# A four-layer network on one core: order of the row blocks in the third layer of the first image, and the place of the second layer of the last image

## The chip, the cores and the metric

The kernel runs on one core of one Trainium2 chip. The metric is the device time of one execution in microseconds (us). Three executions of the kernel before took 2457.15, 2460.21 and 2460.98 us; their median, 2460.21, is the time before.

## The reference

The input is `x`, four images (B = 4) of 64 x 64 places with 64 channels, f32. Four layers follow one another, each of them taking the output of the one before. Cut to what matters:

```python
# layer 0: attention over the 4096 places of an image
q, k, v = x @ Wq + bq, x @ Wk + bk, x @ Wv + bv          # 4096 x 64 each
attn = softmax(einsum('bic,bjc->bij', q, k))             # 4096 x 4096
x = gamma * einsum('bmn,bmc->bnc', attn, v) + x

# layer 1: a gated convolution block
y = dw3x3(pw1(layernorm(x)))                             # 64 -> 256 channels, 3 x 3 per channel
y = y1 * y2                                              # halves of the channels, 128
y = y * (mean(y over places) @ sca_w + sca_b)
x = x + pw2(y) * beta                                    # 128 -> 64
z = pw3(layernorm(x)); z = z1 * z2
x = x + pw4(z) * gamma

# layer 2: attention, on the image read as one matrix without weights
xf = x.reshape(B, C, N)
attn = softmax(einsum('bci,bcj->bij', xf, xf))           # 4096 x 4096, symmetric before the softmax
x = einsum('bcj,bij->bci', xf, attn) + x

# layer 3: attention with 32 inner channels, then a batch norm over all images
f = softmax(theta(x) @ phi(x).T); w_y = (f @ g(x)) @ w_W + w_b
x = x + gamma * (w_y - mean(w_y)) * rsqrt(var(w_y) + eps) + beta    # mean and var over B, H, W
```

## The kernel before

All four images stay on the chip in one array `X` (128 partitions). The program takes its ordinary path in one pass; a second path is there for values out of range only and isn't taken here. The order of the work is written out by hand. `items` is the list of all steps in order: 32 for each image's layer 0, 100 for layer 2 of image 0, 72 for layer 2 of each other image, 64 for each image's layer 3. `due` holds functions that are called after a given item (`at(i, fn)`). Two lanes, `conv` and `misc` (class `Lane`, L995), hold generators; each `yield` names an estimate in us, and `tick(us)` lets the generators go on when their estimated time has come. `run()` (L1831) goes through the items and ticks the lanes. So a lane decides how densely foreign work is put between the steps: each instruction of it stands in its engine's queue behind what was issued before. On TensorE (PE), ScalarE (ACT), VectorE (DVE) and GpSimd (POOL) the program's order is the engine's order; the order of SyncE (SP), which issues most of the DMAs, is left to the tile scheduler.

Layer 1 is the generator `layer1(b)` in the lane `conv`. It starts 34 items after layer 0 of image b has started, so that layer 1 of images 0, 1 and 2 lies beside layer 0 of the next image, and that of image 3 beside layer 2 of image 0. Its parts in order: the first norm (`norm`: squares L1164 on ACT, sums over channels L1170 on PE, L1175, L1176, L1178 and L1179 on ACT and DVE, eight DMAs L1183, a multiplication L1191); twice, for each half of the channels, the first pointwise product (L1205 on PE, L1222 on ACT) into the padded image `pad`, and the convolution in four groups of nine taps, each a 128 x 1024 instruction (L1236 on ACT for the first tap of image 3, L1240 and L1243 on DVE, a product of the halves L1251); the channel weights (L1260); the second pointwise product (L1269 on PE, L1274, L1276); the second norm; the third (L1205, L1286, L1288) and fourth (L1292, L1293, L1295). What follows the taps, from the second norm on, is called the tail of layer 1 below.

Layer 2 (`layer2`, L1322) takes the 4096 x 4096 scores in 8 x 8 blocks of 512. Since the matrix is symmetric, the exponentials of a block serve twice: once for the row block h that is being worked on, and, transposed, for the row block g. PE makes scores from the keys `ko`, which `features2` (L1300) has prepared from X (transposes L1307 on PE, copies L1310 on DVE and ACT, DMAs L1311). One step covers half a block: the score L1384 on PE, two exponentials L1389 on ACT into an `e` buffer, and two or three steps later the products L1440 on PE into two PSUM accumulators. At the end of a row block the accumulators are added to `A` (L1448, L1451, L1454). In a step that belongs to a pair of blocks, `turned` also transposes the exponentials on DVE (L1402) into a buffer `turned`, and `column_sums` adds them up on POOL (image 0: by DMAs that accumulate, L1417; other images: by additions, L1419); the rest is in L1421, L1429 and L1430. When the pair's four steps are done, a *run* follows (`turned_products`): 128 matmuls (L1465) of the turned exponentials with `xr`, a rearranged part of X that `weights` (L1361) has loaded by 16 DMAs of 32 KB, and four additions to `A` (L1478, L1480). The order of row blocks, and where the pairs lie in each, stands in two lists. `FULL`, for images 1 to 3, has 14 runs in 72 steps. `PART`, for image 0, has 7 runs in 100 steps: it works through more blocks directly and turns fewer. In `PART` the runs end at steps 7 and 15, and then, after the 52 steps that hold the row blocks 1 to 4 and most of 7, at 67, 75, 83, 91 and 97. All 100 steps tick the lane `conv` by 3.1 us.

What comes between layer 2 and layer 3 of an image is `close2` (L1517: the sums are gathered and inverted, and A is scaled and added to X), in five turns that are put at given steps of the next image's layer 2; then `open3` (L1560, the projections of layer 3) and `keys3` (L1599, 16 DMAs L1605). Layer 3 (L1610) follows: scores L1627, exponentials L1638, sums L1658 to L1679, products L1688, and `close` (L1744), which writes `wy`; that of images 0 and 1 is kept in the buffer of `pad`.

Buffers: `big` has five (q, v, yg, ko, A, turned and others), `e` six of 2048 columns (two steps each), `t` two, `xn` one (the norms' y and z, xr of images 1 to 3), `pad` one. [...]in layer 2, three slots of two banks go round (`new_ps`, and `piece` for single turns), the fourth holds the accumulators (`new_acc`). A new tile in a buffer waits until the readers of the old one are done.

Of the kernel before, what the change touches and what calls it, by code (L numbers as in the profile page):

```python
# [8 lines left out]
F32 = mybir.dt.float32  # L9
# [682 lines left out]
def fast_path(ctx: ExitStack, tc: tile.TileContext, a: dict, out: bass.AP, bad):  # L692
# [11 lines left out]
    xn = ctx.enter_context(tc.tile_pool(name="xn", bufs=1))  # L704
# [31 lines left out]
    def piece():  # L736
        if turn_of["banks"]:
            return PS[:, bass.ts(new_bank(), 512)]
        return new_ps()[:, 0:512]
# [8 lines left out]
    def new_e(name="e"):  # L748
        return ep.tile([128, 2048], F32, tag="e", name=name)
# [4 lines left out]
    def new_big(name):  # L754
        return big.tile([128, 4096], F32, tag="big", name=name)

    def new_pad(name="pad"):
        return big.tile([128, 66 * PW + 2], F32, tag="pad", name=name, bufs=1)
# [80 lines left out]
    for nm in names64 + names32:  # L839
        n = flat[nm].shape[0]  # L840
# [151 lines left out]
    def at(i, fn):  # L992
        due.setdefault(i, []).append(fn)
# [25 lines left out]
    conv, misc = Lane(), Lane()  # L1019
# [5 lines left out]
    im = [Image() for _ in range(B)]  # L1025
# [49 lines left out]
    between, late, steps, LAG = [], [], [], 6  # L1075
# [5 lines left out]
    def follow(lag=LAG):  # L1081
        if len(late) > lag:
            late.pop(0)()
# [215 lines left out]

    def features2(b):  # L1300
        x = X[:, b]
        im[b].ko = ko = new_big("ko")
        kv = ko[:, 0:N].rearrange("p (a e n) -> p a e n", e=2, n=128)
        for g in range(4):
            ps = piece()
            for i in range(4):
                nc.tensor.transpose(ps[:, bass.ts(i, 128)], x[:, bass.ts(4 * g + i, 128)], ident)  # L1307
            for e, copy in enumerate((nc.vector.tensor_copy, nc.scalar.copy)):
                own, other = slice(64 * e, 64 * e + 64), slice(64 - 64 * e, 128 - 64 * e)
                copy(kv[own, bass.ts(g, 4), e, :], ps[own, :].rearrange("p (a n) -> p a n", n=128))  # L1310
                nc.sync.dma_start(out=kv[other, bass.ts(g, 4), e, :], in_=kv[own, bass.ts(g, 4), e, :])  # L1311
            yield 3.5
# [1 line left out]
    SIDES = [[(7, (h + 1) % 7), ((h + 2) % 7, (h + 3) % 7)] for h in range(7)]  # L1314
    FULL = [(7, [7])] + [(h, [h] + SIDES[h]) for h in range(6)] + [(6, SIDES[6] + [6])]
    PART = [
        (0, [0, 5, (1, 2), 6, 7, (3, 4)]), (1, [1, 2, 3, 4, 7]), (2, [2, 1, 3, 4, 7]), (3, [3, 1, 2, 4]),
        (4, [4, 1, 2, 3]), (7, [7, 0, 5, 6, 1, 2, (3, 4)]), (6, [6, 0, (1, 2), 5, 7, (3, 4)]),
        (5, [5, 0, (1, 2), 6, (3, 4), 7]),
    ]  # L1320

    def layer2(b, when_free=None):  # L1322
# [5 lines left out]
        steps, runs = [], []  # L1328
# [16 lines left out]
        st = {"e": {}, "T": {}, "esum": {}}  # L1345

        def tile_of(run):
            return run % 2 if b else run // (len(runs) - 1)

        def slot(g, t):  # L1350
            k = used[g, t] = used.get((g, t), -1) + 1
# [2 lines left out]

        def weights(h):
            if "xr" not in st:
                st["xr"] = new_e("xr") if b == 0 else xn.tile([128, 2048], F32, tag="xn", name="xn")
            for q in range(4):
                for k in range(4):
                    c = 1024 * (h % 2) + 256 * k  # L1360
                    nc.sync.dma_start(  # L1361
                        out=st["xr"][32 * q : 32 * q + 32, c : c + 256],
                        in_=x[32 * k : 32 * k + 32, 256 * h : 256 * h + 256],
                    )

        if b == 0:
            weights_at = {0: 0, 24: 7, 44: 6, 74: 5}
        else:
            weights_at = {6: 0, 8: 1, **{mine[h][0] - 1: h for h in range(2, 7)}}

        def score(n):
            h, g, u, _, _ = steps[n]
            if n == 0:
                if b > 1:
                    take_slots(0, 1, 2)
                m.zs = sm.tile([128, 216], F32, tag="zs2", name="zs2")
            if n % 2 == 0:
                st["pair"] = new_e()
            e = st["e"][n] = st["pair"][:, bass.ts(n % 2, 1024)]
            ps = new_ps()  # L1380
            for r, c in quads:
                rows_ = slice(64 * r, 64 * r + 64)
                k = 512 * g + 256 * u + 128 * r + 64 * c
                mm(  # L1384
                    ps[64 * c : 64 * c + 64, bass.ts(r, 512)], m.ko[rows_, k : k + 64],
                    m.ko[rows_, bass.ts(h, 512)], start=True, stop=True,
                )
            for r in range(2):
                act(  # L1389
                    e[:, bass.ts(r, 512)], ps[:, bass.ts(r, 512)], AF.Exp, bias=SHIFT2,  # L1390
                    accum_out=slot(g, 2 * u + r),
                )

        def turned(n):
            _, _, _, run, ti = steps[n]
            if run is None:
                return
            k = tile_of(run)
            if k not in st["T"]:
                st["T"][k] = new_big("turned")  # L1400
            T = st["T"][k].rearrange("p (e s j) -> p s e j", e=16, s=8)
            nc.vector.transpose(  # L1402
                T[:, 2 * ti : 2 * ti + 2], st["e"][n].rearrange("p (s e i) -> p s e i", s=2, e=16)
            )

        def column_sums(n):
            h, _, _, run, _ = steps[n]
            if run is None:
                return
            k, e = mine_t[h].index(n), st["e"][n]  # L1410
            if k == (0 if b == 0 else 1):
                st["esum"][h] = new_e("esum")
            if h not in st["esum"]:
                return
            esum = st["esum"][h][:, 0:1024]
            if b == 0:
                nc.gpsimd.dma_start(out=esum, in_=e, **({} if k == 0 else {"accum_op": ALU.add}))  # L1417
            else:
                nc.gpsimd.tensor_add(esum, st["e"][mine_t[h][0]] if k == 1 else esum, e)  # L1419
            if n == mine_t[h][-1]:  # L1420
                nc.gpsimd.tensor_add(esum[:, 0:512], esum[:, 0:512], esum[:, 512:1024])  # L1421

        def spread_sums(h):
            if h == m.mirrored[0]:
                m.cs = sm.tile([128, 128], F32, tag="cs2", name="cs2", bufs=1)
                if b == 0:
                    nc.gpsimd.memset(m.cs, 0.0)
            esum = st["esum"][h]
            nc.vector.transpose(esum[:, 512:1024], esum[:, 0:512])  # L1429
            nc.vector.tensor_reduce(  # L1430
                m.cs[:, bass.ts(h, 16)], esum[:, 512:1024].rearrange("p (e j) -> p e j", j=32), AX.X, ALU.add
            )
# [50 lines left out]
        def item(n):  # L1483
            if n in weights_at:
                weights(weights_at[n])
            score(n)
            turned(n)
            column_sums(n)
            todo.append(n)
            if n == 2:  # L1490
                m.A = new_big("A")
            if b == 0:
                follow(0)
                conv.tick(3.1)
                misc.tick(1.8)
            if n >= late_start:
                for _ in range(2):
                    if todo and todo[0] <= n - (3 if b == 0 and todo[0] in begin else 2):
                        products(todo.pop(0))
            for run, (_, _, last) in enumerate(runs):  # L1500
                if n - (3 if b and run == 0 else 2) == last:
                    turned_products(run)
                    if run == len(runs) - 2 and when_free:
                        when_free()
            if n == len(steps) - 1:
                while todo:
                    products(todo.pop(0))
            if n in spread_at:
                spread_sums(spread_at[n])

        for n in range(len(steps)):
            items.append((lambda n=n: item(n), 1.6 if b else 0.0))
# [281 lines left out]
    conv_from, misc_from, misc_to = {}, {}, {}  # L1794
# [9 lines left out]
    for b in range(B):  # L1804
        misc_to[len(items)] = True
        f = len(items)
        if b == 0:
            layer2(b)
            misc_from[f + 74] = [features2(b + 1)]
        else:  # L1810
            layer2(b, lambda b=b: keys3(b - 1))
            turns = close2(b - 1)
            for i in (8, 12, 22, 32, 42):
                at(f + i, lambda turns=turns: next(turns))
            misc_from[f + 46] = [open3(b - 1)]
            f = len(items)
            misc_to[f] = True
            layer3(b - 1)
            if b + 1 < B:
                turns = features2(b + 1)  # L1820
                for i in (4, 7, 10, 13):
                    between3[f + i] = 2, lambda turns=turns: next(turns)
    f = len(items)
# [220 lines left out]
```

## Time and profile before

| what | value |
|---|---|
| median of three executions | 2460.21 us |
| the profiled execution | 2460.18 us, of which the span of its core is 2458.3 us; mean granted TensorE clock 0.996 |
| PE, 27509 matmuls | 2414.6 us busy |
| DVE, ACT, POOL | 1471.1, 1648.8 and 528.0 us busy |
| 0 to 30 us: load and set-up | 24.0 us PE |
| 30 to 1031: layer 0, with layer 1 of images 0 to 2 | 996.6 us PE, 425.9 DVE, 669.4 ACT |
| 1031 to 1292: layer 2 of image 0, with layer 1 of image 3 | 245.2 us PE, 166.3 DVE, 168.2 ACT, 31.4 POOL |
| 1292 to 1470: layer 2 of image 1 | 177.9 us PE, 119.1 DVE, 82.3 ACT, 121.7 POOL |
| 1470 to 1610: layer 3 of image 0 | 139.0 us PE, 114.6 DVE, 130.7 ACT |
| 1610 to 1790: layer 2 of image 2 | 179.7 us PE, 126.7 DVE, 88.3 ACT, 116.7 POOL |
| 1790 to 2458: the rest | 652.2 us PE, 508.5 DVE, 498.9 ACT, 217.2 POOL |

How to read it. "Busy" is the time in which an engine carries out instructions; a wait is the idle time ahead of an instruction, put down to what released it last. A line of the waits names the engine, what it writes and the line of the program that waited, then, behind an arrow, the engine, its output and the line that it waited for; the three numbers are the us in all, how many times, and the longest one. In a timeline, each line has the start in us, the busy time, engine, line, operation, output and inputs by their names, the size of the tile, and the number of instructions that are taken together; in brackets is the idle time ahead of it and its releaser. In a row of windows, the stretch is followed by its length and by the busy time of each engine with the number of instructions. The tenths of the page cut the span into 40 equal slices of 61.5 us.

### The profile page before, as it was taken

Reading aid. Unit: us, or ns where it says so; the run is one execution under the profiler, and the core shown is the slowest. Engines: PE = TensorE matmul, PEld = TensorE weight load, DVE = VectorE, ACT = ScalarE, POOL = GpSimd, SP = SyncE. Lnnn points to the kernel's source line nnn. Section 1 sums busy time; section 2 is a strip of 40 time slices with the busy share of each in tenths; the row PEclk is TensorE's granted clock in tenths of the full one; section 3 lists DMA queues with packets and bytes.
Section 4 is the critical chain, followed back from the end, with each engine's and each line's share of the span. In section 5 each row is a group of like instructions: output and inputs, shape, how many; then the busy total and the mean of one; then the engine's idle time right before and its main releaser. Section 6 shows DMA issues by size and latency. Waiting matters only on the chain.

```text
span 2458.3 us, 63648 instructions
## 1 busy us (share of the span) xinstructions
PE 2414.6 (98%) x27509; PEld 932.0 (38%) x27509; DVE 1471.1 (60%) x1785; ACT 1648.8 (67%) x3144; POOL 528.0 (21%) x379
## 2 busy tenths in 40 slices
PE   9999999999999999999899999999999999999998
PEld 3343453336433633335334442144431244421113
DVE  2010377227822773278547757877668876678886
ACT  4666766676666666678454449964479844579996
POOL 2000000000000000000127662247631365622110
PEclk9999999999999999999999999999999999999999
DMA  3000000000000000230540017610065400296554
GB/s 79 1 18 1 19 1 18 18 19 1 18 18 18 2 19 18 50 65 18 112 102 22 19 45 155 135 31 19 20 138 118 91 19 20 68 174 139 121 117 117
DMA packets 67094, 134.31 MB, mean 55 GB/s; under 512 B 12941, under 2 KB 34166, under 8 KB 66806
## 3 DMA queue, kind: packets, MB, share of 16 engines
q0 software_dynamic: 23744, 84.46, 17.2%
q1 hardware_dynamic: 42309, 43.85, 7.9%
q8 instruction: 218, 3.57, 0.6%
q10 hardware_dynamic: 752, 1.85, 0.2%
q14 instruction: 71, 0.57, 0.1%
HBM read 4.80 MB, written 4.19 MB: 4 GB/s over the span
## 4 chain that ended last, share of the span: by engine, by line
PE 85%; DVE 7%; ACT 4%; DMA 2%; issue 1%; SPq 0%; POOL 0%; ACTq 0%; DVEq 0%; POOLq 0%
PE PS L1121 18%; PE PS L1095 18%; PE PS L1384 9%; PE PS L1440 9%; PE PS L1627 8%; PE PS L1688 8%; PE PS L1465 7%; PE PS L1205 2%; DVE tg L1679 2%; DVE y L1240 2%; ACT e L1638 2%; DMA xn<-e 1%; ACT e L1389 1%; DVE turned L1402 1%; ACT e L1100 1%
## 5 line engine op out<-in xcount | busy, mean ns | idle before, releaser
L1100 ACT ACTIVATE e<-PS 128x1024 f32<-128x1024 f32 x512 | 523.6, 1023 | 332.3 <-PE PS L1095 299.6
L1389 ACT ACTIVATE e<-PS 128x512 f32<-128x512 f32 x632 | 370.8, 595 | 350.8 <-PE PS L1384 330.6
L1121 PE MATMUL PS<-e,vq 64*64 64x512 f32 x4096 | 577.2, 592 | 0.0
L1095 PE MATMUL PS<-X,q 64*64 64x512 f32 x4096 | 574.9, 590 | 1.8 <-DVE X L979 1.7
L1638 ACT ACTIVATE e<-PS 128x512 f32<-128x512 f32 (+2 forms) x588 | 500.1, 921 | 58.3 <-PE PS L1627 35.8
L1679 DVE TENSOR_TENSOR tg<-tg,e 128x2048 f32<-128x2048 f32 x172 | 393.9, 2290 | 42.8 <-ACT e L1638 31.4
L1384 PE MATMUL PS<-ko 64*64 64x512 f32 x2528 | 343.4, 596 | 2.9 <-DVE A L1480 2.0
L1440 PE MATMUL PS<-e,X 64*64 64x512 f32 x2528 | 339.7, 594 | 1.4 <-DVE X L1133 0.6
L1240 DVE SCALAR_TENSOR_TENSOR y<-pad,vec,y 128x1024 f32<-128x1024 f32 x240 | 307.9, 1283 | 14.8 <-ACT y L1236 7.4
L1419 POOL TENSOR_TENSOR esum<-esum,e 128x1024 f32<-128x1024 f32 x126 | 298.9, 2372 | 49.3 <-ACT e L1389 42.3
L1402 DVE STREAM_TRANSPOSE turned<-e 128x1024 f32<-128x1024 f32 x196 | 241.0, 1238 | 114.0 <-ACT e L1389 114.0
L1627 PE MATMUL PS<-tg,ph 32*64 32x512 f32 x4096 | 294.9, 612 | 1.4 <-ACT e L1638 1.2
L1417 POOL DMA_DIRECT2D esum<-e x28 | 23.1, 827 | 1222.3 <-ACT e L1389 1171.4
L1095 PEld LDWEIGHTS PS<-X,q 64*64 64x64 f32 x4096 | 184.0, 133 | 258.9 <-issue 178.5
L1121 PEld LDWEIGHTS PS<-e,vq 64*64 64x64 f32 x4096 | 184.1, 133 | 252.0 <-issue 158.7
L1688 PE MATMUL PS<-e,tg 128*32 128x512 f32 x2048 | 272.5, 604 | 0.0
L1108 DVE TENSOR_REDUCE sums<-zs 128x1 f32<-128x4 f32 x128 | 19.6, 153 | 260.6 <-ACT e L1100 260.4
L1440 PEld LDWEIGHTS PS<-e,X 64*64 64x64 f32 x2528 | 105.6, 134 | 171.2 <-issue 148.3
L1660 POOL DMA_DIRECT2D xn<-e x116 | 101.1, 897 | 289.9 <-ACT e L1638 205.0
L1384 PEld LDWEIGHTS PS<-ko 64*64 64x64 f32 x2528 | 98.0, 133 | 164.3 <-issue 135.2
L1465 PE MATMUL PS<-turned,xn 32*64 32x256 f32 x5376 | 156.3, 377 | 0.5 <-DVE sums L1534 0.5
L1627 PEld LDWEIGHTS PS<-tg,ph 32*64 32x64 f32 x4096 | 63.4, 129 | 222.5 <-ACT e L1638 191.5
(217 smaller groups left out, 1685.0 us busy)
## 6 DMA issues: line engine op xcount, KB each, us to landing
xn<-e POOLq DMA_DIRECT2D x132, 512.0 KB, 5.2
esum<-e POOLq DMA_DIRECT2D x28, 512.0 KB, 4.6
xn<-X SPq DMA_DIRECT2D x336, 32.0 KB
xn<-t SPq DMA_DIRECT2D x64, 128.0 KB
ph<-tg SPq DMA_DIRECT2D x64, 128.0 KB
ko<-ko SPq DMA_DIRECT2D x32, 128.0 KB
xr<-in_x_dram SPq DMA_DIRECT2D x13, 256.0 KB
q<-q SPq DMA_DIRECT2D x12, 256.0 KB
```

Source lines behind the costliest of these rows:

```text
L1095: mm(ps[64 * c : 64 * c + 64, bass.ts(r, 512)], m.q[rows_, 128 * t + 64 * c : 128 * t + 64 * c + 64], x[rows_, bass.ts(g, 512)], start=Tru ...
L1100: act(es[g // 2][:, bass.ts(g % 2, 1024)], ps, AF.Exp, bias=SHIFT0, accum_out=zs[:, g : g + 1],)
L1121: ins = mm(PS[64 * s : 64 * s + 64, 2048 + 512 * j : 2560 + 512 * j], vq[rows_, :], es[j // 2][rows_, k : k + 512], start=t == 0 and i < 2 ...
L1240: stt(y1, win, wt, y1, ALU.mult, ALU.add)
L1384: mm(ps[64 * c : 64 * c + 64, bass.ts(r, 512)], m.ko[rows_, k : k + 64], m.ko[rows_, bass.ts(h, 512)], start=True, stop=True,)
L1389: act(e[:, bass.ts(r, 512)], ps[:, bass.ts(r, 512)], AF.Exp, bias=SHIFT2, accum_out=slot(g, 2 * u + r),)
L1440: mm(st["acc"][r][64 * c : 64 * c + 64, :], xw[rows_, 4 * g + 2 * u + c, :], st["e"][n][rows_, bass.ts(c, 512)], start=n == mine[h][0], st ...
L1465: mm(slots[q // 2][64 * c : 64 * c + 64, o : o + 256], st["xr"][rows_, w : w + 64], T[rows_, bass.ts(e, 256)], start=e < 2, stop=e >= 14,)
L1627: mm(PS[64 * c : 64 * c + 64, bass.ts(banks[k], 512)], m.ph[32 * k : 32 * k + 32, 128 * mc + 64 * c : 128 * mc + 64 * c + 64], m.th[32 * k ...
L1638: act(e[:, 512 * lo : 512 * k], PS[:, 512 * banks[lo] : 512 * banks[lo] + 512 * (k - lo)], AF.Exp,)
L1679: nc.vector.tensor_add(esum, esum, e)
L1688: mm(st["y"][32 * k : 32 * k + 32, :], m.gx[:, i % 32, :], es[i][:, bass.ts(k, 512)], start=mc == 0, stop=i % 32 == 31,)
```

## The change

Eight edits, all in layer 2 and what lies around it:

1. `ko` of image 1 is put into the buffer of `pad`, not into a `big` buffer.
2. `PART` has a new order: row blocks 0, 1, 7, 2, 6, 3, 5, 4 in place of 0, 1, 2, 3, 4, 7, 6, 5. The parts of each row stay as they are. The 7 runs now end at steps 7, 15, 41, 59, 67, 83 and 89: row blocks with pairs (0, 7, 6, 5) have a row block without any (1, 2, 3, 4) between them.
3. The `turned` tiles of image 0 alternate from run to run, as they do for the other images. Before, the first six runs took one tile and the seventh another.
4. `xr` of image 1 takes an `e` buffer, like that of image 0, and not `xn`.
5. The loads of `xr` for rows 6 and 5 of image 0 are issued at steps 46 and 70 (44 and 74 before); those for rows 0 and 7 stay at 0 and 24.
6. In image 0, a step without a pair ticks the lane `conv` by 2.85 us, and a step with one by 1.2 (3.1 for all before). Since the 100 steps now add up to less, the tail of image 3's layer 1 is left over; `xn` and the lane are taken on into image 1's layer 2, where each step ticks by 1.6 twice.
7. A run of image 0 is put three steps after its last step, not two.
8. `features2(1)` starts at step 89 of image 0's layer 2 (74 before), and the turns of `close2(0)` stand at steps 8, 24, 30, 36 and 42 of image 1's layer 2 (8, 12, 22, 32 and 42 before).

```diff
@@ features2 @@
-        im[b].ko = ko = new_big("ko")
+        im[b].ko = ko = new_pad("ko") if b == 1 else new_big("ko")
@@ layer2's lists @@
     PART = [
-        (0, [0, 5, (1, 2), 6, 7, (3, 4)]), (1, [1, 2, 3, 4, 7]), (2, [2, 1, 3, 4, 7]), (3, [3, 1, 2, 4]),
-        (4, [4, 1, 2, 3]), (7, [7, 0, 5, 6, 1, 2, (3, 4)]), (6, [6, 0, (1, 2), 5, 7, (3, 4)]),
-        (5, [5, 0, (1, 2), 6, (3, 4), 7]),
+        (0, [0, 5, (1, 2), 6, 7, (3, 4)]), (1, [1, 2, 3, 4, 7]), (7, [7, 0, 5, 6, 1, 2, (3, 4)]),
+        (2, [2, 1, 3, 4, 7]), (6, [6, 0, (1, 2), 5, 7, (3, 4)]), (3, [3, 1, 2, 4]),
+        (5, [5, 0, (1, 2), 6, (3, 4), 7]), (4, [4, 1, 2, 3]),
     ]
@@ tile_of @@
-            return run % 2 if b else run // (len(runs) - 1)
+            return run % 2
@@ weights @@
-                st["xr"] = new_e("xr") if b == 0 else xn.tile([128, 2048], F32, tag="xn", name="xn")
+                st["xr"] = new_e("xr") if b < 2 else xn.tile([128, 2048], F32, tag="xn", name="xn")
...
-            weights_at = {0: 0, 24: 7, 44: 6, 74: 5}
+            weights_at = {0: 0, 24: 7, 46: 6, 70: 5}
@@ item @@
-                conv.tick(3.1)
+                conv.tick(2.85 if steps[n][3] is None else 1.2)
...
-                if n - (3 if b and run == 0 else 2) == last:
+                if n - (3 if b == 0 or run == 0 else 2) == last:
@@ the order of the layers @@
-            misc_from[f + 74] = [features2(b + 1)]
+            misc_from[f + 89] = [features2(b + 1)]
...
-            for i in (8, 12, 22, 32, 42):
+            for i in (8, 12, 22, 32, 42) if b > 1 else (8, 24, 30, 36, 42):
```

## The prediction

> **What bounds the kernel now.** I read the page's busy shares first, then TensorE's waits, then the stage with the waits in order of time.
>
> ```profile
> PE 2414.6 (98%) x27509; PEld 932.0 (38%) x27509; DVE 1471.1 (60%) x1785; ACT 1648.8 (67%) x3144; POOL 528.0 (21%) x379
> ...
> PE   9999999999999999999899999999999999999998
> ```
>
> TensorE (PE) is busy 98% of the span, and the change adds and removes no matmul. So it can win only what PE idles, or runs slowly, in the stages that it touches. One digit is below 9 before the end: the slice from 1168 us. Stage by stage (columns: window, length, then PE, PEld, DVE, ACT, POOL busy, granted clock, DMA share, GB/s):
>
> ```profile
> 1031.00:1175.00 144.00, 134.04 (x1417) 61.62 (x1416) 114.56 (x118) 104.46 (x292) 11.25 (x14) 0.98 0.26 55
> 1175.00:1292.00 117.00, 111.19 (x1356) 43.85 (x1344) 51.78 (x73) 63.73 (x173) 20.12 (x21) 0.97 0.53 108
> 1292.00:1470.00 178.00, 177.92 (x2934) 85.45 (x2930) 119.09 (x161) 82.28 (x261) 121.72 (x55) 1.00 0.12 29
> ```
>
> The first two windows are layer 2 of image 0, with layer 1 of image 3 beside it; the third is layer 2 of image 1. Image 0 leaves PE idle 9.96 + 5.81 = 15.8 us, image 1 0.1 us. VectorE (DVE) is loaded unevenly: 80% in the first window, 44% in the second. The waits behind those 15.8 us:
>
> ```profile
> PE PS L1465 <- DVE turned L1402: 6.5, 1, 6.5
> ...
> PE PS L1205 <- ACT e L1389: 2.1, 1, 2.1
> PE PS L1384 <- DVE A L1480: 2.0, 1, 2.0
> PE PS L1292 <- DVE u L1288: 1.7, 1, 1.7
> ...
> PE PS L1170 <- ACT sq L1164: 1.2, 1, 1.2
> ```
>
> The largest, in order of time, PE and then DVE:
>
> ```profile
> 1165.79 1.12 PE L1440 MATMUL PS<-e,X 64*64 64x512 f32 x8
> 1173.37 6.42 PE L1465 MATMUL PS<-turned,xr 32*64 32x256 f32 x128 [6.45 <-DVE turned L1402]
> ```
>
> ```profile
> 1167.28 2.56 DVE L1240 SCALAR_TENSOR_TENSOR y<-pad,vec,y 128x1024 f32<-128x1024 f32 x2
> 1169.76 1.24 DVE L1402 STREAM_TRANSPOSE turned<-e 128x1024 f32<-128x1024 f32 x1
> 1170.92 1.24 DVE L1240 SCALAR_TENSOR_TENSOR y<-pad,vec,y 128x1024 f32<-128x1024 f32 x1
> 1172.08 1.23 DVE L1402 STREAM_TRANSPOSE turned<-e 128x1024 f32<-128x1024 f32 x1
> ```
>
> DVE has had no gap of over 0.1 us since 1122; its convolution taps (L1240) stand ahead of the transposes (L1402) that the third run needs. The same L1465 group takes 3.71 us undisturbed (at 1205.47) and 6.42 after the idle time: 2.7 us more.
>
> **What the Trainium skill says.** TensorE: Matmul & The Clock Gate, "What's actually happening": an idle PE falls back to half clock after a window of about 3.4 us. The 6.42 for 3.71 agrees; but here 1.98 us of idle at 1072 also cost about 1.75 (1.29 + 3.45 for 1.09 + 1.90 us of the same groups) and 2.08 us at 1223 about 1.95, so I charge shorter gaps too. The same page, "Architectural detail: the array is 16× 32×32, not 1× 128×128": ACT and DVE are strict FIFO; the lines above show it. PSUM — Partial Sum Buffer, "PSUM bank collisions raise a hardware error": two engines on one bank must be guarded; here ACT's copies at L1310 waited 5.0 us (three waits) for DVE's on the same bank. DMA: Bandwidth & Descriptors, "Issuing engines are not separate DMA queues": initiating a DMA is usually small beside it. This trace differs: SP needed 7.79 us for 8 issues of L1183 and 23.54 for 32 of L1361, with a median of 0.60 and 0.58 each.
>
> **Part 1, spaced runs and slower ticks.** Units from the timeline: a step (L1384 + L1440) is 1.72 us of PE, a run (L1465) 3.64, a pointwise group 0.86; on DVE a tap is 1.31, a transpose 1.16 back to back, four A adds 1.35, an L1251 or L1454 pair 1.23 to 1.33. Before, the second and third run are 52 steps apart: 89.4 + 3.6 + 8 groups (6.9) = 100 us of PE against all 72 tap instructions' worth (89) and some 17 of other work on DVE: 6 late, as seen. After, the instruction order gives, run to run: 2nd to 3rd PE 48, DVE 37; 3rd to 4th PE 38, DVE 28 plus about 7 in which it waits for ACT to refill the pad (7.45 in the trace); 4th to 5th 17.4 against 15.5; 5th to 6th 31.2 against 31.5 (15 taps 19.7, four transposes 4.6, the rest 7.2); 6th to 7th 15.8 against 12.6. No run waits but perhaps the sixth: 0.5 us, bounds 0 to 2. Gone: 6.45 + 2.7 = **9.2**. The wait at 1072 goes as well: there L1480, which empties the second run's two PSUM slots, stood behind five taps (6.53 us); after, no tap precedes it. 1.98 + 1.75 = **3.7**. SP's weights of image 0, 16 issues (9.6 us) each from steps 46 and 70, are needed by runs at 62 and 86, 27 us and more later: nothing. The third step of grace before a run (3 for 2) costs nothing: the wait moves behind one more step, and DVE has already finished with the first runs.
>
> **Part 2, the tail of layer 1 goes to image 1.** The second norm, pw3 and pw4 leave image 0's layer 2, and with them the waits at L1170, L1205 and L1292: 1.17 + 0.96 (L1170 slow, 2.00 for 1.04) + 2.08 + 1.95 + 1.71 = **7.9** gone there. Their work (about 12 us on DVE, 10 on ACT) fits beside image 1: 119 and 82 of 178. But the chain returns. Two squares (2.0 on ACT) delay the last exp of image 0: 0.9. From L1170 the chain is L1175, L1176, L1178, L1179, eight DMAs on SP, one multiply; before, L1205 came 19.4 us after L1170 and waited. Counting from the end of L1170, PE now has 13 groups (11.2 us) before L1205; L1179 ends after 3.5, four DMAs (2.4) and their landing (4, as from the last issue to L1191 in the trace) take it to 9.9, the multiply waits for one transpose and ends at about 12.5: 1.3 of wait. The expensive part is SP: xr of image 1 now takes an e buffer whose last reader is image 0's last product, and its first 16 DMAs stand behind those eight. With 0.6 each: 3.5 + 24 x 0.6 = 17.9, landing 2 to 4: 20 to 22, against PE's first run at 12.5 + 8 groups = 19.4, which L1288 behind two transposes may hold back too: 2.5 us, bounds 0 to 6. Clock 2. Sum **+6.7**, bounds 2 to 12. Below nothing it can't go: image 1 has no idle time to give.
>
> **Part 3, keys of image 1 in the pad, later (step 89 for 74).** The first transpose (L1307) holds one of three PSUM slots until DVE's L1310, which stands behind four transposes, taps, and an L1251 pair, and ACT's copy follows it. From the sixth run: DVE reaches L1310 after 13.6 and 0.7 us, ACT is done at 14.9; PE wants that slot at 11.7. That's 3.2 us of wait, clock 1.8: **+5**, bounds 0 to 7 (0 if DVE is a step ahead, more if it brings lag). The last keys' DMAs have some 9 us to spare before image 1's first score. The pad is free for wy only after image 1; its next user comes a layer later, at no cost.
>
> **Part 4, the e pool.** xr takes one of six e buffers through image 1. Each pair that reuses a buffer read by POOL does so 8 steps or more after the read was queued, except steps 16, 26 and so on, which follow POOL's seventh add of the group before; the trace has that add 9 us ahead of that exp. Nothing, covered by those 9 us; the later close2 turns and keys3's earlier place in SP's queue likewise: 16 issues of 0.6 end before the weights behind them are free to load.
>
> **Sum.** −9.2 − 3.7 − 7.9 + 6.7 + 5 + 0.5 = −8.6. The profiled execution took 2460.18 us (span 2458.3), the median is 2460.21, so no correction: 2460.2 − 8.6 = **2452**.
>
> **Rivals.** *Most of it is won* (2443): DVE is ahead at the copies (part 3: 1) and xr lands in time (part 2: 3): −20.8 + 4 = −17. For: the 9 and 6 us of slack in early stretches; against: the in-order queue resets it at each run. *Given back* (2458): part 2 at SP's 0.74 each of 23.54/32 (10), part 3 at 7, the sixth run 2: −20.8 + 19 = −2. For: both waits are new and each follows from the order; against: POOL's DMAs, in flight in that row, are finished by then. *Slower, SP as bound* (2467): at L1183's 0.97 each, 24 issues take 23.3, run one waits 11 and the second weights (40 issues, 38.8) hold the next pair 6, with two clock drops 5: part 2 becomes 22, the sum +6.7. It decides from about 0.9 us an issue. *The runs wait as before*: only if DVE's order were kept, which the instruction order excludes, or taps took over 1.6 us; then about 2461, counted with the third.
>
> **Chances.** The forecast (2449 to 2456) 0.50, most won 0.15, given back 0.20, SP 0.15. A measurement tells about 0.2%, 4.9 us, from none. Faster takes most won and nine tenths of the forecast: 0.60; slower is SP: 0.15; same 0.25. Range: from most won to short of SP's 2467, 2443 to 2464.
>
> **What would show it.** Right: no L1465 wait on turned above 1 us; none on A L1480; PE idle of 1 to 4 us at L1384 between the sixth and seventh run, and at L1205 or the first L1465 of image 1. Wrong: a long wait of that L1465 on SP's xr; ACT's L1389 waiting for POOL in image 1; stage times (image 0 some 14 less, image 1 some 6 more) that don't shift so.

## The result, and the profile after

The changed kernel took 2475.6 us (median of six, 2469.6 to 2477.0) against 2458.8 before: a ratio of 1.0065, 95% interval 1.0052 to 1.0078. It is slower by 0.65%, some 17 us, where 8.6 faster were forecast. Its profiled execution took 2474.17 us, with a span of 2472.4, 14.1 more than before.

The whole of it lies in the two stages that the change touches. The first score of layer 3 starts at 1484.83 us, and at 1470.70 before. The windows below are layer 2 of image 0 and of image 1, cut within 0.4 us of image 1's first score (columns: window, length, then PE, PEld, DVE, ACT, POOL busy, granted clock, DMA share, GB/s), first before, then after:

```profile
1018.00:1277.60 259.60, 244.30 (x2762) 105.50 (x2758) 164.31 (x190) 167.54 (x458) 26.18 (x31) 0.97 0.37 77
1277.60:1470.70 193.10, 192.54 (x3052) 89.88 (x3044) 124.64 (x166) 92.82 (x292) 126.90 (x58) 1.00 0.14 33
```

```profile
1018.00:1263.20 245.20, 230.60 (x2664) 91.30 (x2660) 153.61 (x181) 158.93 (x447) 28.36 (x33) 0.98 0.38 78
1263.20:1484.80 221.60, 210.31 (x3150) 96.68 (x3142) 143.99 (x175) 101.73 (x302) 127.33 (x56) 0.98 0.14 33
```

The tail has moved: PE's work falls by 13.7 and rises by 17.8. PE's idle time in image 0, though, has hardly changed (15.3 before, 14.6 now), and image 1, which had 0.6, has 11.3. The other 4.1 us (230.60 + 210.31 against 244.30 + 192.54) are the same matmuls at a lower clock after the waits. PE's waits in both stages:

```profile
PE PS L1465 <- DVE turned L1402: 12.9, 5, 4.2
PE PS L1170 <- DVE X L1133: 3.9, 1, 3.9
PE PS L1205 <- DVE xn L1191: 2.4, 1, 2.4
...
PE PS L1384 <- ACT ko L1310: 1.6, 1, 1.6
```

The waits at L1384 on A, at L1292, and at L1170 on sq are gone or below 0.3 us, as forecast. The wait of the runs for their transposes has doubled, and L1170 has one that no step of the prediction names. In order of time:

```profile
1031.79 1.94 PE L1170 MATMUL PS<-X,jsel 128*32 128x512 f32 x8 [3.94 <-DVE X L1133]
...
1124.20 5.23 PE L1465 MATMUL PS<-turned,xr 32*64 32x256 f32 x128 [3.08 <-DVE turned L1402]
...
1219.42 5.51 PE L1465 MATMUL PS<-turned,xr 32*64 32x256 f32 x128 [2.89 <-DVE turned L1402]
...
1353.02 4.10 PE L1465 MATMUL PS<-turned,xr 32*64 32x256 f32 x128 [1.43 <-DVE turned L1402]
1366.61 3.71 PE L1465 MATMUL PS<-turned,xr 32*64 32x256 f32 x128 [1.27 <-DVE turned L1402]
1386.21 5.61 PE L1465 MATMUL PS<-turned,xr 32*64 32x256 f32 x128 [4.24 <-DVE turned L1402]
```

Before, the first of these lines and the additions to X that it waits for stood in the other order:

```profile
1026.29 1.06 PE L1170 MATMUL PS<-X,jsel 128*32 128x512 f32 x8
```

```profile
1031.79 1.37 DVE L1133 SCALAR_TENSOR_TENSOR X<-PS,gam,X 128x512 f32<-128x512 f32 x2
```

Three things are to be seen. First, the norm of image 3 (L1170, at 1031.79) now waits for two of layer 0's last four additions to X (L1133). The trace has 16 of these, four for each image, so the last four are all that layer 0 adds to image 3. The reference takes the norm after them. The kernel before takes the norm's sums over channels ahead of all four, and the changed kernel ahead of two; the squares (L1164) are taken ahead of all four in both. So the place that costs nothing is one at which the data are not yet complete. Second, the third and sixth run of image 0 still wait. Third, three runs of image 1, which had no wait at all, wait 6.94 us, and the last of them takes 5.61 us where 3.71 is usual. DVE ahead of the two runs of image 0, and POOL beside it:

```profile
1085.35 0.71 DVE L1429 STREAM_TRANSPOSE esum<-esum 128x512 f32<-128x512 f32 x1 [8.98 <-POOL esum L1421]
...
1198.14 0.71 DVE L1429 STREAM_TRANSPOSE esum<-esum 128x512 f32<-128x512 f32 x1 [7.71 <-POOL esum L1421]
```

```profile
1190.87 0.87 POOL L1417 DMA_DIRECT2D esum<-e  x1 [4.21 <-ACT e L1389]
1196.85 1.26 POOL L1421 TENSOR_TENSOR esum<-esum 128x512 f32<-128x512 f32 x1 [5.10 <-DMA esum<-e]
```

DVE stands still for 8.98 and 7.71 us. The sums of a row block come from a chain of accumulating DMAs on POOL, each waiting for the one before (5.0 to 5.4 us from one to the next in the chain that ends at 1196.85, up to 6.7 in the one ahead of 1085.35), and L1429 is put five steps after the row block's last pair step, before the chain is through. All taps behind it, and so the next run's transposes, come later by that. And ahead of the last wait of image 1, on DVE:

```profile
1378.64 1.22 DVE L1543 TENSOR_TENSOR t<-PS,rz 128x1024 f32<-128x1024 f32 x1
1379.89 5.11 DVE L1549 TENSOR_TENSOR X<-X,t 128x512 f32<-128x512 f32 x2
1384.92 3.48 DVE L1402 STREAM_TRANSPOSE turned<-e 128x1024 f32<-128x1024 f32 x3
```

A turn of close2 (L1543, two L1549) takes 6.3 us and stands ahead of the last of the four transposes that the run needs: the first of the three L1402 in that line, which ends at 1386.17. The other two belong to the next run.

### The profile page after: what moved, and what is told of

Its sections match the earlier page's. It is cut to its first block, busy times and chain, and to the rows that moved or that the text cites. A ratio compares the mean times of both kernels' runs of the same rounds, so it can differ in the third digit from the quotient of the medians.

```text
span 2472.4 us, 63644 instructions
## 1 busy us (share of the span) xinstructions
PE 2419.0 (98%) x27509; PEld 924.9 (37%) x27509; DVE 1480.3 (60%) x1785; ACT 1648.8 (67%) x3144; POOL 530.6 (21%) x379
## 4 chain that ended last, share of the span: by engine, by line
PE 83%; DVE 9%; ACT 5%; issue 2%; DMA 0%; SPq 0%; POOL 0%; DVEq 0%; ACTq 0%; POOLq 0%
PE PS L1095 17%; PE PS L1121 17%; PE PS L1627 8%; PE PS L1384 8%; PE PS L1440 8%; PE PS L1688 8%; PE PS L1465 8%; DVE tg L1679 3%; PE PS L1205 2%; DVE y L1240 2%; ACT e L1638 2%; ACT e L1389 1%; DVE turned L1402 1%; PE PS L1170 1%; ACT e L1100 1%
## 5 line engine op out<-in xcount | busy, mean ns | idle before, releaser
L1638 ACT ACTIVATE e<-PS 128x512 f32<-128x512 f32 (+2 forms) x588 | 499.8, 921 | 58.5 <-PE PS L1627 36.7
L1384 PE MATMUL PS<-ko 64*64 64x512 f32 x2528 | 342.9, 598 | 1.7 <-ACT ko L1310 1.6
L1440 PE MATMUL PS<-e,X 64*64 64x512 f32 x2528 | 336.5, 592 | 4.8 <-ACT e L1389 1.9
L1240 DVE SCALAR_TENSOR_TENSOR y<-pad,vec,y 128x1024 f32<-128x1024 f32 x240 | 308.4, 1285 | 16.9 <-ACT y L1236 10.0
L1402 DVE STREAM_TRANSPOSE turned<-e 128x1024 f32<-128x1024 f32 x196 | 240.3, 1237 | 100.2 <-ACT e L1389 99.9
L1627 PE MATMUL PS<-tg,ph 32*64 32x512 f32 x4096 | 294.8, 613 | 0.9 <-ACT e L1638 0.8
L1440 PEld LDWEIGHTS PS<-e,X 64*64 64x64 f32 x2528 | 99.8, 133 | 181.0 <-issue 154.9
L1384 PEld LDWEIGHTS PS<-ko 64*64 64x64 f32 x2528 | 92.6, 132 | 169.2 <-issue 141.1
L1627 PEld LDWEIGHTS PS<-tg,ph 32*64 32x64 f32 x4096 | 63.5, 129 | 221.8 <-ACT e L1638 189.1
L1389 ACT ACTIVATION_READ_ACCUMULATOR e<-PS 128x1 f32 x632 | 127.6, 202 | 0.0
```

What stands on the lines that cost most here:

```text
L1240: stt(y1, win, wt, y1, ALU.mult, ALU.add)
L1384: mm(ps[64 * c : 64 * c + 64, bass.ts(r, 512)], m.ko[rows_, k : k + 64], m.ko[rows_, bass.ts(h, 512)], start=True, stop=True,)
L1389: act(e[:, bass.ts(r, 512)], ps[:, bass.ts(r, 512)], AF.Exp, bias=SHIFT2, accum_out=slot(g, 2 * u + r),)
L1440: mm(st["acc"][r][64 * c : 64 * c + 64, :], xw[rows_, 4 * g + 2 * u + c, :], st["e"][n][rows_, bass.ts(c, 512)], start=n == mine[h][0], st ...
L1627: mm(PS[64 * c : 64 * c + 64, bass.ts(banks[k], 512)], m.ph[32 * k : 32 * k + 32, 128 * mc + 64 * c : 128 * mc + 64 * c + 64], m.th[32 * k ...
L1638: act(e[:, 512 * lo : 512 * k], PS[:, 512 * banks[lo] : 512 * banks[lo] + 512 * (k - lo)], AF.Exp,)
```

## Experiments

My theory was that three slips, each in the place of one step, cost all of it: the norm's place, the stall at L1429, and the turns. Its rival was one shared bound, DVE's queue, in which a wait only moves. All ratios are to the kernel before, with 95% intervals.

**1. The turns back.** `for i in (8, 12, 22, 32, 42):` for image 1 as well, the rest as changed.

> The changed kernel with the turns of close2(0) at steps 8, 12, 22, 32 and 42 of image 1 again. Theory A (the turns stand too close: each puts 4.6 to 6.3 us of L1543 and L1549 ahead of the transposes L1402, every 6 steps): the waits of the runs at 1353, 1367 and 1386 us (1.43 + 1.27 + 4.24, and some 2.3 of slow clock after them) go, 9 us; the turn at step 12 meets the tail of layer 1 and gives back 1 to 3: 2467 to 2469 us. Theory B (the tail's own work on DVE is what the transposes stand behind, the turns only show it): the waits move to the runs of steps 12 to 30 and the sum stays, 2473 to 2477.

2466.35 us, ratio 1.0031 (1.0020 to 1.0042), 9.3 less than the change. The three waits of image 1 are gone; one of 0.88 us, behind the tail's L1288, has come. Theory A. Image 0 is as in the change here, and its sixth run still waits 1.28 us where the change's trace has 2.89 (in experiment 7, where it is the same too, 2.88, and the third run 3.59 for 3.08). So a single wait differs by as much as 1.6 us from one execution to the next, and small differences of waits between two traces show nothing.

**2. The first ticks back.**

```diff
-                conv.tick(2.85 if steps[n][3] is None else 1.2)
+                conv.tick(3.1 if n < 8 else 2.85 if steps[n][3] is None else 1.2)
```

> The changed kernel with ticks of 3.1 us in the first 8 steps of image 0, as before, and the slower ticks after that. Theory A (the slower ticks let the first norm of image 3 slip past two of the last additions of layer 0, L1133, so that L1170 must wait for them): L1170's wait of 3.94 us and the 1.8 us of slow clock after it go, and nothing comes back: 2469 to 2471 us. Theory B (PE would wait there anyway, for X at L1440 and for the exponentials, as in the kernel before with 0.6 + 0.6): 2 us or less are won, 2473 to 2476.

2462.17 us, ratio 1.0013 (1.0007 to 1.0020): 13.4 less, far more than either theory said. L1170's wait is gone, but the tail also stands 8.6 us of lane time earlier (8 x 3.1 less 4 x 2.85 and 4 x 1.2). Experiment 8 tries to part the two.

**3. The sums later.**

```diff
-        spread_at = {mine_t[h][-1] + 5: h for h in m.mirrored}
+        spread_at = {mine_t[h][-1] + (5 if b else 9): h for h in m.mirrored}
```

> The changed kernel with L1429 and L1430 of image 0 put nine steps after the last pair step of a row block, not five. Theory A (DVE stands idle for 8.98 and 7.71 us at L1429, since POOL's chain of accumulating DMAs, 5.1 us each, ends late, and the taps behind it then reach the third and the sixth run's transposes late): both stalls go or fall below 2 us, and with them the waits of these runs, 3.08 + 1.52 and 2.89 + 1.80 of slow clock: 2465 to 2468 us. Theory B (the taps are simply too dense ahead of these runs): DVE's stalls go, but each run still waits 2 us or more, 2473 to 2476.

2473.43 us, ratio 1.0056 (1.0042 to 1.0070), which can't be told from the change (1.0052 to 1.0078); the time lies where theory B put it. In the profiled execution, which took 2470.88 us, the mechanism is as theory A has it. DVE has no stall, and the runs wait 0.39 us and not at all:

```profile
1090.88 0.70 DVE L1429 STREAM_TRANSPOSE esum<-esum 128x512 f32<-128x512 f32 x1
...
1195.31 0.70 DVE L1429 STREAM_TRANSPOSE esum<-esum 128x512 f32<-128x512 f32 x1
```

```profile
1121.79 3.71 PE L1465 MATMUL PS<-turned,xr 32*64 32x256 f32 x128 [0.39 <-DVE turned L1402]
...
1212.66 3.71 PE L1465 MATMUL PS<-turned,xr 32*64 32x256 f32 x128
```

Layer 3 starts 5.9 us earlier than in the change's trace. By its time alone this run settles nothing; experiments 4 and 5 do.

**4. All three edits.**

> The three edits together. Theory A (three separate causes): the gains add, 8 + 5 + 9 = 22 us at most, and some of it lost since the tail comes some 9 us of lane time earlier: 2453 to 2458 us. Theory B (one shared bound, DVE's queue, to which each wait only moves): no better than the best single one, 2465 or more.

2446.58 us, ratio 0.9947 (0.9934 to 0.9960): the gains add, below theory A's range, and with 29.0 us they come to more than the 24.9 of the three runs singly. This version is faster than both kernels. No run waits; what is left of PE's waits in the two stages is 6 to 7 us:

```profile
PE PS L1205 <- DVE A L1478: 2.2, 1, 2.2
PE PS L1205 <- ACT e L1389: 1.0, 1, 1.0
PE PS L1440 <- ACT own L1451: 1.0, 1, 1.0
```

**5. The turns and the first ticks, but not the sums.**

> The turns back (8, 12, 22, 32, 42) and ticks of 3.1 us in the first 8 steps, but L1429 and L1430 at five steps again. Theory A (the stall of DVE at L1429 is a cause of its own): the third and sixth run wait 1.5 to 3 us again, and the time stands 4 to 8 us above the 2446.6 of the three edits together: 2451 to 2455 us. Theory B (with the taps earlier in the queue the stall has no price): 2446 to 2449.

2452.51 us, ratio 0.9975 (0.9966 to 0.9983). L1429 stalls DVE for 6.15 and 9.00 us again, and the third and sixth run wait 2.70 and 1.45. The place of the sums is worth 5.9 us here, and the intervals of 4 and 5 don't touch. Theory A.

**6. The tail left in image 0**: as 4, but `conv.tick(3.1)` in all steps.

> As with the three edits together, but with ticks of 3.1 us in all 100 steps of image 0, so that the tail of layer 1 (second norm, L1205, L1292) lies in image 0's layer 2 again, as in the kernel before; the new order of row blocks, ko in pad and the later keys stay. Theory A (spreading the tail over image 1 is worth what its waits cost in image 0 before, 7.9 us, less 2 that come back): 2451 to 2455 us. Theory B (what is won comes from the order of row blocks alone; the tail costs as much in either place): 2445 to 2449.

2455.40 us, ratio 0.9988 (0.9982 to 0.9995). That is 8.8 us above 4, at the edge of theory A's range. The faster ticks also set the taps closer together, so the 8.8 us are the price of both: all of layer 1 in image 0, and at a denser pace. PE waits there at the fourth run and at the channel weights, which lie among or just behind the taps, and at the tail:

```profile
1159.23 5.61 PE L1465 MATMUL PS<-turned,xr 32*64 32x256 f32 x128 [2.57 <-DVE turned L1402]
...
1181.67 0.56 PE L1260 MATMUL PS<-ytot,sca 128*128 128x1 f32 x2 [3.79 <-DVE ytot L1257]
...
1221.87 1.21 PE L1205 MATMUL PS<-xn,pw 64*64 64x512 f32 x8 [2.08 <-ACT e L1389]
```

**7. POOL's additions left out in image 1**, on the changed kernel.

```diff
-            else:
+            elif b != 1 or k == 1:
                 nc.gpsimd.tensor_add(esum, st["e"][mine_t[h][0]] if k == 1 else esum, e)
```

> The changed kernel with all but the first addition of each row block's column sums in image 1 left out (L1419), so image 1's sums lack these terms; POOL has then some 85 us less to do there. Theory A (L1549 and L1191 take 1.6 to 2.8 us where 0.7 and 1.2 are usual because POOL adds at the same time, and that makes the close turns so costly): L1549 falls to 0.7 and L1191 to 1.2, a turn takes some 2.6 us in place of 4.6 to 6.3, the waits of the three runs fall from 6.9 to below 2.5 in sum, L1205's from 2.36 to below 1: 2465 to 2469 us. Theory B (these instructions are slow for another reason, such as PE's reading of X): they stay above 1.5 us and the waits above 5: 2472 to 2477.

2465.06 us, ratio 1.0028 (1.0017 to 1.0039), 10.5 less: theory A. The groups that read X on DVE in that stage (duration in ns: least, median, most), first in the changed kernel, then here:

```profile
L1549 DVE TENSOR_TENSOR X<-X,t x8: 693/1986/2747, 1344.8 to 1401.1; 128x512 f32<-128x512 f32 x8
...
L1191 DVE TENSOR_TENSOR xn<-xn,X x2: 2372/2870/3368, 1281.0 to 1283.3; 128x1024 f32<-128x1024 f32 x2
```

```profile
L1549 DVE TENSOR_TENSOR X<-X,t x8: 691/692/2734, 1343.6 to 1392.2; 128x512 f32<-128x512 f32 x8
...
L1191 DVE TENSOR_TENSOR xn<-xn,X x2: 1183/1198/1214, 1282.4 to 1283.5; 128x1024 f32<-128x1024 f32 x2
```

L1549 falls from 1.99 to 0.69 us in the median; only the first turn, beside the addition that was kept, still has one of 2.73. The runs wait 1.93 us in sum for 6.94, L1205 waits 1.17 for 2.36. The Trainium skill, SBUF — State Buffer, "Who interferes with whom", says that a DVE instruction with two SBUF inputs contends with a GpSimd instruction that reads SBUF. The trace agrees: L1549 and L1191 have two such inputs and are stretched, L1543, with one input in PSUM, takes 1.18 to 1.22 us beside POOL as well, and L1402, with one input, 1.25.

**8. The norm's place alone**: ticks of 3.1 for n < 8 and 2.31 for 16 to 31, else as changed.

> The changed kernel with ticks of 3.1 us in the first 8 steps of image 0 and of 2.31 in steps 16 to 31, so that the first norm stands where it did before, and everything from the taps on where the change puts it. Theory A (of the 13.4 us that the early ticks won, the norm's wait is 3.94 + 1.8 less the 0.6 that comes back, and the rest came from a tail that starts earlier): 2469 to 2471 us. Theory B (all of it is the norm): 2461 to 2464. Theory C (DVE, not the norm, bounds that stretch: the third run waits longer by what the norm wins): 2473 or more.

2463.93 us, ratio 1.0023 (1.0015 to 1.0031), 11.7 less: theory B. Of the 13.4 of experiment 2, the place of the norm, with what follows it up to step 31, is nearly all; from step 32 on the lane stands as in the change. The norm costs more than its own wait, for everything behind it is late: L1191 starts at 1044.09 us here and at 1061.67 in the changed kernel, the pad is filled 13 to 19 us later there, and the first L1240 starts at 1086.77 for 1068.74. The third run has no wait here. So its 3.08 us, and the 1.52 of slow clock after it, come from the norm's place together with the stall at L1429: experiment 3 leaves the norm where the change has it and brings that wait down to 0.39. For this run the two prices can't be added.

**9. The turns alone, on the kernel before**: (8, 24, 30, 36, 42) for image 1.

> The kernel before with one part of the change alone: the turns of close2(0) at steps 8, 24, 30, 36 and 42 of image 1. Theory A (turns 6 steps apart, each 2.7 us of additions where POOL is idle and up to 5 beside it, hold up the transposes whatever else lies in image 1): two or three runs wait on turned again, 5 to 9 us slower than before: 2463 to 2467 us. Theory B (they only hurt because the tail of layer 1 fills DVE's queue as well): within 2 us of before, 2457 to 2460.

2469.98 us, ratio 1.0042 (1.0028 to 1.0056), 11.5 more than before: theory A, by more than it allowed. With no tail in image 1, the same three runs wait as long as in the changed kernel:

```profile
1348.35 3.93 PE L1465 MATMUL PS<-turned,xn 32*64 32x256 f32 x128 [1.43 <-DVE turned L1402]
1361.77 3.71 PE L1465 MATMUL PS<-turned,xn 32*64 32x256 f32 x128 [1.28 <-DVE turned L1402]
...
1381.37 6.75 PE L1465 MATMUL PS<-turned,xn 32*64 32x256 f32 x128 [4.25 <-DVE turned L1402]
```

**10. The norm's slip alone, on the kernel before**: the change's ticks for n < 8, then 3.64 in steps 16 to 31 to make them good.

> The kernel before with the ticks of the change in the first 8 steps of image 0 alone (2.85 and 1.2), made good by ticks of 3.64 in steps 16 to 31, so that the first norm of image 3 slips behind two of L1133 and the rest of the lane stands as before. Theory A (the slip costs its own wait, 5.7 us less 0.6, and holds back the filling of pad, so that the third run's taps end later still): 2465 to 2471 us, with the third run's wait longer than 6.45. Theory B (DVE makes good the delay before the third run): 2462 to 2464. Theory C (the wait is hidden in this kernel): within 2 us of before.

2464.80 us, ratio 1.0026 (1.0016 to 1.0036), 6.3 more than before. L1170 waits 3.94 us, and the third run 7.10 for 6.45, so the time is near theory B's end while the longer wait is theory A's. The slip costs 6 here and 12 in the changed kernel, where the third run comes 26 steps after the second and not 52.

**11. Turns far apart but in the midst of pairs, on the kernel before**: (8, 16, 26, 36, 45) for image 1.

> The kernel before with the turns of close2(0) at steps 8, 16, 26, 36 and 45 of image 1: the last four are nine or ten steps apart, as before, but each stands at the second or third step of a pair, where before (12, 22, 32, 42) each stood at the first step of a row block, whose two steps have no transposes and no addition on POOL. Theory A (the place decides: in the midst of a pair a turn delays transposes that the next run needs, and POOL's additions stretch L1549): waits of 1 to 4 us on turned at two to four runs and L1549 above 1.2 us each, 2464 to 2478 us. Theory B (only the distance of 6 steps did it, DVE having no time to catch up): no such wait above 0.5 us, 2457 to 2461 us.

2479.37 us, ratio 1.0091 (1.0077 to 1.0104), 22 more than before. Theory A, a little above its range: a distance of 6 steps isn't needed. Three runs wait 4.25 us each, and 1.76 us of the loss is another cost, of the last turn at step 45: open3's L1570 waits for its L1549. Two of the runs:

```profile
1329.12 5.61 PE L1465 MATMUL PS<-turned,xn 32*64 32x256 f32 x128 [4.25 <-DVE turned L1402]
...
1361.30 6.59 PE L1465 MATMUL PS<-turned,xn 32*64 32x256 f32 x128 [4.25 <-DVE turned L1402]
```

The old places 12, 22, 32 and 42 are the first steps of row blocks, without transposes and with little on POOL: there L1549 has a median of 0.76 us. Here it has 2.54.

**12 and 13. The old order of row blocks**, all else as in 4. In 12 one thing went wrong: the seventh run's last pair step is 97, and three steps later there is no step, so that run (128 matmuls and four additions) is left out. 13 keeps it, two steps after.

> As with the three edits together, but with the row blocks of image 0 in the old order (0, 1, 2, 3, 4, 7, 6, 5) and the loads of xr at the old steps 44 and 74; all other parts of the change and the three edits stay. Theory A (the new order is what takes the third run's wait away: between the second and the third run lie the taps of 52 steps again, and the last runs stand close together): the third run waits 4 to 7 us and PE slows after it, 2453 to 2460 us. Theory B (the slower ticks alone thin out the taps enough): within 2 us of the three edits together, 2445 to 2449 us.

> As the kernel with the old order of row blocks and the three edits, but with the seventh run of image 0 kept, two steps after its last pair step (the run before this one left it out: 128 matmuls, 3.7 us of PE, and four additions to A). Theory A (the order matters little, the ticks do the work): no wait on turned at the third run, and 2449.6 + 3.7 and up to 2 us of waits near the seventh: 2452 to 2456 us, so the new order is worth 6 to 9 us, at the end of image 0, not at the third run. Theory B (the left-out run had hidden nothing): 2447 to 2451 us, and the order is worth 3 or less.

2449.61 us, ratio 0.9965 (0.9952 to 0.9979), and 2450.88, ratio 0.9967 (0.9955 to 0.9979). In both the third run starts without a wait, so the new order isn't needed to take its wait away. The slower ticks are the likely cause, but they weren't tried alone on the kernel before. With the new order and the old ticks (experiment 6) the third run doesn't wait either; there the fourth does. 13 stands 4.3 us above 4, between its two theories, and the two intervals just overlap. It waits at the end of image 0, 5.1 us at L1440 on L1448. The new order is thus worth some 4 us, not sharply known, and not at the third run.

## Why the prediction was wrong

Experiment 5 is the change without two slips, and takes 2452.5 us; 2452 was forecast. What the forecast left out is +9.7 for the turns (2462.17 with them, 2452.51 without) and +13.4 for the first ticks (2475.6 and 2462.17). The agreement is in part luck, as the points show.

- **"The later close2 turns ... likewise" (part 4, set at nothing): this step failed, 9.7 us.** I asked which buffers and which SP issues a later turn meets, and not what stands in DVE's queue there. A turn at step 24, 30 or 36 is queued among the transposes of a pair, and its L1549 runs beside POOL's additions. Experiments 1, 9 and 11 show the place as cause, 7 the stretching.
- **"Spaced runs and slower ticks" (part 1): the ticks' first effect was not listed, 11.7 us.** I followed the slower ticks where they were meant to act, between the runs, and not at the lane's first instruction. In the kernel before, L1170 is queued ahead of layer 0's last four L1133 and reads X without waiting, and without what they add; now it stands behind two of them. Experiments 2, 8 and 10 show the price. What a norm behind all four would cost, no run shows.
- **The third run's 9.2 us, gone, and 0.5 for the sixth: wrong in the change, right once the slips are out.** 3.08 + 1.52 and 2.89 + 1.80 were left. I had set DVE's 37 us of work against PE's 48, which held (1086.8 to 1124 without a gap), but let DVE start at the second run. It started 10 us later, behind L1429's wait of 8.98 on POOL, which the list of durations doesn't contain since it is idle time. In experiment 4 no run waits. The norm's late start is the other half of it (experiment 8). Nor was the spacing of the runs, to which I gave the credit, needed: experiment 13 has the old order and no wait at the third run.
- **The wait at 1072 (3.7) and the tail's waits in image 0 (7.9): right**; none of the four (L1384 on A, L1170 on sq, L1205, L1292) is left in image 0 above 0.3 us.
- **Part 2, the tail in image 1 (+6.7): size right, parts wrong.** L1205 waits 2.36 us for 1.3, since the first L1191 ahead of it takes 2.37 us beside POOL for 1.2. The first run of image 1, charged 2.5 for xr and SP, has no wait; 1.43 at L1440 on L1448, not forecast, stands there. That the work "fits beside image 1" by its sum was no argument: DVE was busy 19.4 us longer there, where I had counted 12.
- **Part 3, the keys (+5): 1.64 us.** PE waited for L1310 once, by half of what was worked out.
- **The rival on the slower side was SP.** No wait on xr or on SP's weights appears at any run. The result is slower by another mechanism, at which the rivals did not look. Nor does this trace differ where I wrote that it does: 0.60 us to issue a DMA is small beside the 4 us that I took for its landing.
- **The range, up to 2464,** took its bounds from the terms that were listed. A part set at nothing had no upper bound.

That an edit was made for a good reason and costs 29 us by three slips is shown by experiments 4, 5 and 2 in turn: 5.9 + 9.7 + 13.4. (The kernel before, timed beside each, had medians of 2458.2 to 2459.7; by the ratios to it the three are 6.9, 9.3 and 12.8.) These are differences along one order of undoing; in another the shares differ (9.3 for the turns alone, about 2 for the sums alone).

Open is why the sums alone won so little in the timed runs (2.2 us) when its trace shows both stalls and both waits gone. The 2.5 us lost again after 1479 us in its trace don't explain it: they go with one wait of layer 3 (L1627 on L1638, 1.35 us at 2222.94), which the traces of 4 and 5 have too (1.51 and 1.70) and that of the change does not, and 5 lacks this edit.

## What to carry to other kernels

A pace that is changed moves every instruction of its lane: compare the two orders from the lane's first instruction on, and ask of each that has moved what it is now queued behind. Ask, too, of one that doesn't wait, whether its data are complete there. An in-order engine's wait is paid by all that stands behind it, so a step's price is its time and the idle time ahead of it. Put additions whose inputs both lie in SBUF where POOL is idle and no run is near, and price them by a row from such a place, not by the mean of all.

## What the runs showed of the hardware

- The same 128x512 addition on DVE (L1549) took 0.69 us with POOL idle and up to 2.84 (experiment 11) beside POOL's 128x1024 additions of 2.36 us; a 128x1024 one (L1191) took 1.20 and up to 3.37.
- Accumulating DMAs of 512 KB, issued one after another by POOL, followed each other every 5.0 to 5.4 us (1159.82 to 1190.87 in the changed kernel); eight of them set the time of a row block's sums.
- The price after a wait isn't set by its length alone: after 2.89 us of idle time the sixth run took 5.51 us in the changed kernel and 3.92 in experiment 8, where 3.71 is usual; after 1.43 us it was 4.10, after 1.27 3.71, after 4.25 5.41 to 6.75.
